# Expert weights in buffers of gathered rows: a separate chain of weight loads in a mixture-of-experts stage

## The chip, the cores and the metric

The kernel runs on one NeuronCore of a Trainium2 chip. The metric is the device time of one execution in microseconds. The kernel before takes 3864.81 us, the median of 3 runs (3861.73 to 3865.3). One more execution was profiled; it took 3860.75 us.

The engines of the core each work through their own list of instructions in order and wait for each other with semaphores: TensorE (PE) for matrix products and transposes, VectorE (DVE), ScalarE (ACT), GpSimd (POOL), which here issues all indexed transfers (gathers and scatters of rows), and SyncE (SP), which issues the plain transfers.

## The reference

Four layers follow each other on the same graph: 3125 nodes with 256 features, 50,000 edges. Each layer adds a graph part and then a feed-forward part to x. The change lies in the third layer (and, in part, in the fourth):

```python
x = x + _L2_gnn_ref(_layernorm(x), edge_attr_64, node_vec1, src, dst, W_self, W_func, W_att)
x = x + _L2_ffn_ref(_layernorm(x)[None], gate_w, gate_b, w1, b1, w2, b2, gamma, beta)[0]
```

The graph part is attention over edges. With z = h·W_func, an edge's score is a leaky ReLU of a linear function of z[src], z[dst] and an edge value; a softmax over the edges of each target node gives the weights with which the rows z[src] are summed; then come W_self, a ReLU and the sum with h. The feed-forward part is a mixture of 16 experts, of which each node takes 2:

```python
topk_vals, topk_idx = top_k(x @ gate_w + gate_b, 2);  topk_w = softmax(topk_vals)
h = relu(einsum('bsh,ehf->bsef', x, w1) + b1)          # f = 512
y = x + sum_k topk_w[k] * (h @ w2 + b2)[expert topk_idx[k]]
out = (y - mean(y)) / sqrt(var(y) + 1e-5) * gamma + beta
```

The fourth layer's graph part projects x with a ReLU, takes the maximum over each node's incoming edges, and adds two products and a batch norm; its feed-forward part is again a mixture, of 8 experts, 2 for each node. All is float32.

## The kernel before, in words

**Tiles.** The nodes are sorted by their number of edges and cut into 25 tiles of 128. The features of all of them stay in on-chip memory (`X`, `XX`, `ACC`). The gathered edge rows don't: an edge row is 258 floats, and one POOL instruction (`gather`, recorded at L136) fetches one row for each of 128 nodes. Tile t takes `RND[t]` such gathers; all tiles together take 413.

**The third layer's stage** (L2099 to L2303) has five strands, each a Python generator that yields the engine and an estimated duration of its next piece:

- `gathers()` on POOL fetches the edge rows for the tiles in `order2` (24 down to 6, then 0 to 5) into tiles named `g_rows`, four gathers each, in nine buffers (`GR_BUFS`), that is room for 36 gathers. A buffer comes free when DVE has added its last row (L2222).
- `attend()` does the softmax and the weighted sum of each tile, mainly on DVE.
- `route2()` does norm, gate logits, top 2 and positions in six groups, and scatters each node's row to its two experts' places in a table `xg` in HBM (POOL, L140).
- `ex2.loads()` on SP fetches tokens and weights for the experts.
- `experts2()` runs the experts chunk by chunk. Chunk 0 is tiles 15 to 24, chunk 1 tiles 6 to 14, chunk 2 tiles 0 to 5, the last to be gathered. Each chunk runs all 16 experts on a fixed number of places (2 × 96 in the first two, 128 in the last): transposes of the tokens (L1989, copied to `ro_xt` at L1994 on ACT or L1997 on DVE), the first product `mm` (L1947), the activation into `ro_h`, the second product `y` (L1951) and a store to the table `yg` in HBM (L2033).

After that a flag is read back and a branch taken if an expert's places overflowed (`ex2.rest`, L2036; here none do). Then `ex2.fetch` gathers each node's two results from `yg` (buffers `ro_g`, a ring of six), and `table3` in six groups of tiles (20–24, 15–19, 10–14, 6–9, 3–5, 0–2) combines them (L2093), norms, projects on PE for the fourth layer (L1734, L2265, L2267), applies the ReLU and scatters the rows to a table `tab3`, from which the fourth layer gathers. The end of chunk 2's experts and all of this run interleaved.

**What sets the order.** A list scheduler (`Plan`) walks the strands and writes all engines' instructions down in an order of its own, from the estimated durations, the ranks of the strands and objects that stand for buffers (`Ring`) and moments (`At`, `All`). The estimate only decides the order. Once written, each engine executes its list in that order, and real semaphores guard the data.

**The loads before.** For each chunk and expert, `loads()` (L1953) issues on SP, as one chain: the tokens (L1962), once a token buffer is free (`XR`, two) and all of the chunk's scatters are out (`sent[c]`); then the two halves of the expert's weights (L1968), 514 and 512 KB, each once one of its two buffers (`W_BUFS`) is free. So a chunk's first weights stand behind its first tokens. The fourth layer's stage (experts in chunks of tiles 0–4, 5–14 and 15–24) uses the same method.

Of the kernel before, what the change touches and what calls it, by code (L numbers as in the profile page):

```python
# [9 lines left out]
F32 = mybir.dt.float32  # L10
# [9 lines left out]
P = 128  # L20
# [4 lines left out]
D = 256  # L25
# [8 lines left out]
GB = 4  # L34
GR_BUFS = 9
ROWS = 24
W_BUFS = 2
GT = 5
# [26 lines left out]
ZW = D + 2  # L65
# [30 lines left out]
def tile_gnn_ffn(ctx: ExitStack, tc: tile.TileContext, a: dict, out: bass.AP):  # L96
    nc = tc.nc
# [1509 lines left out]
    X, XN = XX[:, :, V_X : V_X + D], XX[:, :, V_N : V_N + D]  # L1607
    ACC = np_.tile([P, NT, D], F32, name="ACC")
    xi = np_.tile([P, NT], I32, name="xi")
    lg2 = np_.tile([P, GT, 16], F32, name="lg2")  # L1610

    def turned(dst, src, scale=None, bias=None):

# [135 lines left out]
    plan = [None]  # L1749
# [60 lines left out]
    class Experts:  # L1810
# [3 lines left out]
        def __init__(self, key, n, act, chunks, pool, xg, yg, scale=None, bias=None):  # L1814
            self.n, self.act, self.chunks, self.pool, self.xg, self.yg = n, act, chunks, pool, xg, yg
            self.scale, self.bias = scale, bias
            self.f, self.fc, self.blocks = 512, 512 // P, a[key + "_blocks"]
            self.b2 = pool.tile([n, D], F32, name="ro_b2")
            nc.sync.dma_start(self.b2, a[key + "_b2"])

            self.base, self.trash = [], []
            for c, (t0, t1, m, k) in enumerate(chunks):
                e = pool.tile([P, n], F32, name=f"ro_e{c}")
                nc.vector.tensor_scalar(e, iota_f[:, :n], float(m * k), float(n * m * k), op0=OP.mult, op1=OP.subtract)
                tr = pool.tile([P, 2, t1 - t0], F32, name=f"ro_t{c}")
                nc.vector.tensor_scalar(tr.rearrange("p i t -> p (i t)"), iota_f[:, : 2 * (t1 - t0)], float(P), iota_p,
                                        op0=OP.mult, op1=OP.add)
                self.base.append(e)
                self.trash.append(tr)
            self.big = max(P, *(q[2] * q[3] for q in chunks))  # L1830
            self.bk = max(q[3] for q in chunks)
            self.back = pool.tile([P, 2, NT], I32, name="ro_back")
            self.pos = pool.tile([P, 2, NT], I32, name="ro_pos")
            self.w = pool.tile([P, 2, NT], F32, name="ro_w2")
            self.left = pool.tile([P, NT, n], F32, name="ro_left")
            self.sofar = [pool.tile([P, n], F32, name=f"ro_r{c}") for c in range(len(chunks))]
            for r in self.sofar:
                nc.vector.memset(r, 0.0)
            self.over = pool.tile([P, 1], F32, name="ro_over")
            nc.vector.memset(self.over, 0.0)  # L1840
            self.W, self.XR = (Ring(W_BUFS), Ring(W_BUFS)), Ring(2)
            self.there, self.came = [], [At() for _ in range(len(chunks) * n)]
            self.sent = [All(t1 - t0) for t0, t1, _, _ in chunks]
            self.made = [At() for _ in chunks]
            self.G, self.got, self.back_in = Ring(6), [[] for _ in range(NT)], [At() for _ in range(NT)]
            self.placed = [At() for _ in range(NT)]
# [103 lines left out]
            for i in range(self.fc):  # L1950
                nc.tensor.matmul(py, h[:, i, s], w[:, i * D : (i + 1) * D], start=(i == 0), stop=(i == self.fc - 1))  # L1951

        def loads(self):  # L1953

            pool, half = self.pool, 2 * self.f + self.fc
            for c, (_, _, m, k) in enumerate(self.chunks):
                for e in range(self.n):
                    r0 = e * m * k
                    f = yield "SP", 0.45, (self.XR, self.sent[c])
                    xfree = self.XR.take()  # L1960
                    x = pool.tile([P, self.bk, D], F32, name="ro_x", bufs=2)[:m, :k]
                    nc.sync.dma_start(x, self.xg[c][r0 : r0 + m * k, :].rearrange("(k p) d -> p k d", p=m))  # L1962
                    parts = [(x, plan[0].moved(f, m * k * 1024), xfree)]
                    for i, ring in enumerate(self.W):
                        f = yield "SP", 0.45, (ring,)
                        wfree = ring.take()
                        w = pool.tile([P, half if i == 0 else self.fc * D], F32, name=f"ro_w{i}", bufs=W_BUFS)
                        nc.sync.dma_start(w, self.blocks[e * P : (e + 1) * P, half * i : half + i * self.fc * D])  # L1968
                        parts.append((w, plan[0].moved(f, 0.53e6), wfree))
                    self.there.append(parts)  # L1970
                    self.came[len(self.there) - 1].t = f

        def run(self, c, R):

            pool, (_, _, m, k) = self.pool, self.chunks[c]
            cols = m * k

            def turn(e):
                at = c * self.n + e
                while self.came[at].t is None:  # L1980
                    yield None, 0.0, (self.came[at],)
                x, xl, xfree = self.there[at][0]
                xt = pool.tile([P, 2, self.big], F32, name="ro_xt", bufs=2)[:, :, :cols]
                for q in range(2):
                    f = yield "PE", 0.13 * k, (xl, R["tp"])
                    free = R["tp"].take()
                    pt = ps("tp", [P, 512])
                    for i in range(k):
                        nc.tensor.transpose(pt[:, i * m : (i + 1) * m], x[:, i, q * P : (q + 1) * P], ident[:m, :m])  # L1989
                    if q:  # L1990
                        xfree.t = f
                    f = yield ("ACT" if self.scale is not None else ("ACT", "DVE")), 0.15 + cols * 0.0011, (f,)
                    if self.scale is not None:
                        nc.scalar.activation(xt[:, q, :], pt[:, :cols], AF.Identity, bias=self.bias[:, q : q + 1],  # L1994
                                             scale=self.scale[:, q : q + 1])
                    else:
                        (nc.scalar.copy if plan[0].on == "ACT" else nc.vector.tensor_copy)(xt[:, q, :], pt[:, :cols])  # L1997
                    free.t = f
                return xt, f

            xt, xf = yield from turn(0)
            for e in range(self.n):
                (w1, wl1, free1), (w2, wl2, free2) = self.there[c * self.n + e][1:]
                h = pool.tile([P, self.fc, self.big], F32, name="ro_h", bufs=2)[:, :, :cols]
                for i in range(self.fc):
                    f = yield "PE", 2 * cols * MM_COL, (wl1, xf, R["mm"])
                    free = R["mm"].take()
                    ph = ps("mm", [P, 512])[:, :cols]
                    self.hidden(w1, xt, ph, i)
                    f = yield "ACT", 0.2 + cols * 0.0011, (f,)  # L2010
                    j = 2 * self.f + i
                    nc.scalar.activation(h[:, i, :], ph, self.act, bias=w1[:, j : j + 1])  # L2012
                    free.t = f
                hf = free1.t = f
                if e + 1 < self.n:
                    xt, xf = yield from turn(e + 1)
                y = pool.tile([P, self.bk, D], F32, name="ro_y", bufs=2)[:m, :k]
                for i0 in range(0, k, 2):
                    g = min(2, k - i0)
                    for i in range(g):  # L2020
                        f = yield "PE", self.fc * D * MM_COL, (hf, wl2, *((R["y"],) if i == 0 else ()))
                        if i == 0:
                            free = R["y"].take()
                            py = ps("y", [P, 2, D])[:m, :g]
                        self.out_of(py[:, i, :], w2, h, slice((i0 + i) * m, (i0 + i + 1) * m))
                    if i0 + g == k:
                        free2.t = f
                    f = yield ("ACT", "DVE"), 0.15 + 0.27 * g, (f,)
                    (nc.scalar.copy if plan[0].on == "ACT" else nc.vector.tensor_copy)(y[:, i0 : i0 + g, :], py)  # L2029
                    free.t = f  # L2030
                r0 = e * cols
                f = yield "SP", 0.45, (f,)
                nc.sync.dma_start(self.yg[c][r0 : r0 + cols, :].rearrange("(k p) d -> p k d", p=m), y)  # L2033
            self.made[c].t = f + 0.5
# [64 lines left out]
    with tc.tile_pool(name="g2", bufs=2) as gp, \  # L2099
# [179 lines left out]
        with tc.manual_schedule(engines={EN.PE, EN.DVE, EN.Activation, EN.Pool, EN.SP}):  # L2279
            pl.add(2, gathers())  # L2280
            pl.add(0, attend())
            pl.add(1, route2())
            pl.add(0, ex2.loads())
            last = pl.add(4, experts2())
            pl.run(moved, R.values())
            ex2.rest(range(NT))
# [11 lines left out]
    with tc.tile_pool(name="w3", bufs=1) as wp:  # L2298
# [70 lines left out]
        with tc.tile_pool(name="f3", bufs=1) as fp, psums(tp=2, mm=2, y=2, u=2):  # L2369
# [50 lines left out]
            with tc.manual_schedule(engines={EN.PE, EN.DVE, EN.Activation, EN.Pool, EN.SP}):  # L2420
                for i, q in enumerate(groups3):
                    befores.append(At())
                    pl.add(i, route3(*q, f"f{i % 2}_", befores[i], befores[i + 2]))
                pl.add(0, ex3.loads())
                pl.add(1.5, experts3())
                pl.run(routed, R.values())
                ex3.rest(range(NT))
# [59 lines left out]
```

## Time and profile before

| | |
|---|---|
| median of 3 runs | 3864.81 us |
| profiled execution: its time, its span | 3860.75 us, 3859.0 us |
| busy share of the span: PE, DVE, POOL, ACT | 71%, 51%, 45%, 22% |
| mean granted clock of PE | 0.82 |
| third layer: last gather of edge rows starts | 2709.32 us |
| third layer: chunk 2's tokens are loaded from | 2749.82 us |
| third layer: chunk 2's last expert output ends on PE | 2882.2 us |
| third layer: last scatter to the fourth layer's table ends | 2936.65 us |
| fourth layer: first gather of edge rows | 2943.27 us |
| fourth layer: first tokens loaded | 3515.13 us |

Times within the execution are microseconds from the start of its span. Busy time of an engine doesn't count waits or the issuing of plain transfers. A line of the timeline gives start, length, engine and source line, what it writes and reads, and in brackets how long the engine was idle before it and what ended that.

### The profile page before, as it was taken

The page shows a single profiled execution, that of the slowest core. Times are in us where ns is not written, and L with a number is a line of the kernel's source. Part 1 is how long each engine was busy: PE and PEld are TensorE (multiplying, and loading weights), DVE is VectorE, ACT ScalarE, POOL GpSimd, SP SyncE. Part 2 cuts the span into 40 slices and gives each one's busy share as a digit, 9 for nine tenths or more (in the row PEclk, how much of TensorE's full clock was granted, in tenths as well). Part 3 has the DMA queues.
Part 4 walks back from the last instruction along what each step waited for, and adds up shares of the span by engine and source line. Part 5 has one row for each costly group of instructions (what it writes and reads, how often), then busy time and mean ns, then how long its engine had stood idle before and what let it go on. Part 6 is the DMA issues. An engine that isn't in the chain of part 4 may idle for free. (4 is left out here: it accounts for less than half of the span.)

```text
span 3859.0 us, 46777 instructions
## 1 busy us (share of the span) xinstructions
PE 2721.7 (71%) x13015; PEld 2250.7 (58%) x13015; DVE 1987.3 (51%) x7555; ACT 846.0 (22%) x1771; POOL 1724.6 (45%) x1971
## 2 busy tenths in 40 slices
PE   3788999999899999999384227748483112237994
PEld 2666788887788888887373115537361111225673
DVE  4446665776566555544423755656664333337411
ACT  2111232322122322323121002213231000014331
POOL 0342233352144333330024777777435777762343
PEclk9778999998899999999687557869695555557997
DMA  5756544553243444431122437768452333333563
GB/s 181 235 157 208 165 136 128 153 159 84 67 120 94 137 115 122 116 109 47 49 87 73 110 104 241 212 185 261 161 172 76 105 105 105 105 93 116 172 212 97
DMA packets 274479, 518.31 MB, mean 134 GB/s; under 512 B 53068, under 2 KB 176106, under 8 KB 274194
## 3 DMA queue, kind: packets, MB, share of 16 engines
q0 software_dynamic: 103744, 303.34, 26.9%
q1 hardware_dynamic: 159598, 201.27, 16.9%
q10 hardware_dynamic: 10852, 10.45, 0.8%
q8 instruction: 113, 1.85, 0.2%
q14 instruction: 172, 1.41, 0.1%
HBM read 428.07 MB, written 86.78 MB: 133 GB/s over the span
## 5 line engine op out<-in xcount | busy, mean ns | idle before, releaser
L136 POOL DMA_INDIRECT g<-tab,m_si x521 | 499.1, 958 | 1013.7 <-PE agg L884 262.4
L136 POOL DMA_INDIRECT g_rows<-tab,srcI x413 | 401.7, 973 | 130.6 <-issue 101.8
L136 POOL DMA_INDIRECT g_row<-tab,srcI x413 | 391.0, 947 | 132.2 <-issue 118.1
L866 PEld LDWEIGHTS c<-s,g 128*128 128x128 f32 x2084 | 332.5, 207 | 95.6 <-issue 38.7
L897 PE MATMUL f<-w_rel,aT 128*126 128x256 f32 x1600 | 377.2, 385 | 0.0
L866 PE MATMUL c<-s,g 128*128 128x96 f32 x2084 | 334.2, 286 | 51.2 <-DMA g<-tab,m_si 21.6
L870 ACT COPY aT<-c 128x384 f32<-128x384 f32 (+1 forms) x273 | 230.0, 842 | 607.0 <-PE c L866 573.4
L873 PE MATMUL pw<-w_d,f 65*128 65x256 f32 x1042 | 354.1, 424 | 0.0
L2342 DVE TENSOR_TENSOR ACC<-ACC,g_row 128x256 f32<-128x256 f32 x413 | 175.7, 425 | 341.5 <-DMA g_row<-tab,srcI 340.9
L884 PE MATMUL agg<-g,s 128*126 128x256 f32 x1042 | 334.1, 403 | 5.4 <-DVE g L875 5.4
L897 PEld LDWEIGHTS f<-w_rel,aT 128*126 128x126 f32 x1600 | 302.3, 191 | 48.3 <-issue 4.0
L1617 PE MATMUL tp<-ident,ACC 128*128 128x128 f32 x50 | 16.6, 435 | 422.3 <-DVE ACC L2342 422.3
L1947 PE MATMUL mm<-ro_xt,ro_w 128*128 128x192 f32 (+3 forms) x1152 | 265.0, 378 | 46.8 <-ACT ro_h L2012 25.0
L875 DVE TENSOR_TENSOR g<-pw,g 128x256 f32<-128x256 f32 x521 | 218.9, 420 | 120.0 <-PE pw L873 117.5
L1951 PE MATMUL y<-ro_w,ro_h 128*96 128x256 f32 (+2 forms) x1152 | 267.3, 384 | 0.0
L1617 PEld LDWEIGHTS tp<-ident,ACC 128*128 128x128 f32 x50 | 7.2, 204 | 429.8 <-issue 354.1
L1947 PEld LDWEIGHTS mm<-ro_xt,ro_w 128*128 128x128 f32 x1152 | 200.6, 205 | 95.0 <-ACT ro_h L2012 33.0
L884 PEld LDWEIGHTS agg<-g,s 128*126 128x126 f32 x1042 | 211.4, 203 | 40.2 <-DVE g L875 5.8
L1951 PEld LDWEIGHTS y<-ro_w,ro_h 128*96 128x96 f32 (+2 forms) x1152 | 200.2, 179 | 43.5 <-issue 1.0
L1015 PE MATMUL w<-w,b_h 128*126 128x256 f32 x800 | 211.7, 389 | 3.5 <-ACT xt L928 1.7
L1006 PE MATMUL w<-xt,w 128*128 128x252 f32 (+1 forms) x832 | 206.8, 372 | 3.0 <-ACT b_h L1008 1.3
L2222 DVE SCALAR_TENSOR_TENSOR ACC<-g_rows,g_e,ACC 128x256 f32<-128x256 f32 x413 | 201.5, 488 | 13.6
(582 smaller groups left out, 4674.2 us busy)
## 6 DMA issues: line engine op xcount, KB each, us to landing
ro_w<-in_L_ffn_blocks SPq DMA_DIRECT2D x72, 514.0 KB
ro_w<-in_L_ffn_blocks SPq DMA_DIRECT2D x72, 512.0 KB
f<-in_attr_t SPq DMA_DIRECT2D x521, 32.5 KB
xg<-zero SPq DMA_DIRECT2D x78, 200.0 KB
b_at<-in_edge_attr SPq DMA_DIRECT2D x100, 125.0 KB
tabr<-v SPq DMA_DIRECT2D x12, 758.0 KB
g<-tab,m_si POOLq DMA_INDIRECT x521
g_rows<-tab,srcI POOLq DMA_INDIRECT x413
```

What stands on the lines that cost most here:

```text
L136: return nc.gpsimd.indirect_dma_start(out=dst, out_offset=None, in_=table, in_offset=bass.IndirectOffsetOnAxis(ap=idx, axis=0))
L866: nc.tensor.matmul(pc[:, h, o : o + GW], g[:, h * P : (h + 1) * P], sums[k][0], start=True, stop=True)
L870: nc.scalar.copy(aT[:, :, :, b : b + n * GN].rearrange("p k r n -> p k n r"), pc[:, :, : n * GW].rearrange("p k (n r) -> p k n r", r=16))
L873: nc.tensor.matmul(pw, feats.pop(k), wd, start=True, stop=True)
L875: nc.vector.tensor_tensor(g[:, D:], pw, g[:, D:], op=OP.mult)
L884: nc.tensor.matmul(cur["agg"][:TN], sums.pop(k)[1], rows.pop(k)[:, D:], start=(j == 0), stop=last)
L897: nc.tensor.matmul(cur["f"][:TN], aT[:, h, r, :], wrel[:, h, r, :], start=(r == 0 and h == 0), stop=(r == 15 and h == 1))
L1006: nc.tensor.matmul(ph, w["01"][:, e, k, i * P : (i + 1) * P], xt[:, k, : n * TN], start=(k == 0), stop=(k == 1))
L1015: nc.tensor.matmul(py, last[:, k, i * TN : (i + 1) * TN], w["02"][:, e - 1, k, :], start=(k == 0), stop=(k == 1))
L1947: nc.tensor.matmul(ph, w[:, o : o + P], xt[:, k, :], start=(k == 0), stop=(k == 1))
L1951: nc.tensor.matmul(py, h[:, i, s], w[:, i * D : (i + 1) * D], start=(i == 0), stop=(i == self.fc - 1))
L2222: stt(u, g[:, r, :D], e[:, r0 + r : r0 + r + 1], u, op0=OP.mult, op1=OP.add)
```

## The change

The loads are cut into two strands. `tokens()` issues the token loads, with the same conditions as before. `weights()` issues the weight loads, which wait only for a buffer: no longer for the tokens of the same expert, nor for the chunk's scatters. `run()` waits, in the plan, for each of the two separately.

For the third layer, `weights()` is given a second source of buffers: in the last chunk, from the third expert on, each half goes into a tile of the name `g_rows`, viewed as 128 × 1032 floats and cut to the half's width. In the plan such a load waits for a buffer of that ring and for the moment when the last row gather was issued (`here[order2[-1]]`). That gives 28 loads into nine buffers, about 4.5 experts deep, beside the two experts in the ordinary buffers. The fourth layer calls `weights()` without it. A tile of logits that nothing used is gone.

```diff
-        def loads(self):
-
-            pool, half = self.pool, 2 * self.f + self.fc
+        def tokens(self):
+
             for c, (_, _, m, k) in enumerate(self.chunks):
                 for e in range(self.n):
-                    r0 = e * m * k
+                    r0, at = e * m * k, c * self.n + e
                     f = yield "SP", 0.45, (self.XR, self.sent[c])
-                    xfree = self.XR.take()
-                    x = pool.tile([P, self.bk, D], F32, name="ro_x", bufs=2)[:m, :k]
+                    free = self.XR.take()
+                    x = self.pool.tile([P, self.bk, D], F32, name="ro_x", bufs=2)[:m, :k]
                     nc.sync.dma_start(x, self.xg[c][r0 : r0 + m * k, :].rearrange("(k p) d -> p k d", p=m))
-                    parts = [(x, plan[0].moved(f, m * k * 1024), xfree)]
-                    for i, ring in enumerate(self.W):
-                        f = yield "SP", 0.45, (ring,)
-                        wfree = ring.take()
-                        w = pool.tile([P, half if i == 0 else self.fc * D], F32, name=f"ro_w{i}", bufs=W_BUFS)
-                        nc.sync.dma_start(w, self.blocks[e * P : (e + 1) * P, half * i : half * i + self.fc * D])
-                        parts.append((w, plan[0].moved(f, 0.53e6), wfree))
-                    self.there.append(parts)
-                    self.came[len(self.there) - 1].t = f
+                    self.there[at] = x, plan[0].moved(f, m * k * 1024), free
+                    self.came[at].t = f
+
+        def weights(self, more=None):
+
+            half = 2 * self.f + self.fc
+            for c in range(len(self.chunks)):
+                for e in range(self.n):
+                    for i in range(2):
+                        n = (half, self.fc * D)[i]
+                        if more and c + 1 == len(self.chunks) and e >= W_BUFS:
+                            ring, make, since = more
+                            f = yield "SP", 0.45, (ring, since)
+                            w = make()[:, :n]
+                        else:
+                            ring = self.W[i]
+                            f = yield "SP", 0.45, (ring,)
+                            w = self.pool.tile([P, n], F32, name=f"ro_w{i}", bufs=W_BUFS)
+                        free = ring.take()
+                        nc.sync.dma_start(w, self.blocks[e * P : (e + 1) * P, half * i : half * i + n])
+                        at = (c * self.n + e) * 2 + i
+                        self.loaded[at] = w, plan[0].moved(f, 0.53e6), free
+                        self.fetched[at].t = f
...
-            pl.add(0, ex2.loads())
+            pl.add(0, ex2.tokens())
+            pl.add(0, ex2.weights((blocks, lambda: gp.tile([P, GB, ZW], F32, name="g_rows", bufs=GR_BUFS)
+                                   .rearrange("p r d -> p (r d)"), here[order2[-1]])))
...
-                pl.add(0, ex3.loads())
+                pl.add(0, ex3.tokens())
+                pl.add(0, ex3.weights())
```

More of the change, by code (lines that the diff above doesn't have):

```diff
@@ L1609, in tile_gnn_ffn @@
     xi = np_.tile([P, NT], I32, name="xi")
-    lg2 = np_.tile([P, GT, 16], F32, name="lg2")
     def turned(dst, src, scale=None, bias=None):
@@ L1841, in __init__ @@
             self.W, self.XR = (Ring(W_BUFS), Ring(W_BUFS)), Ring(2)
-            self.there, self.came = [], [At() for _ in range(len(chunks) * n)]
+            self.there, self.came = {}, [At() for _ in range(len(chunks) * n)]
+            self.loaded, self.fetched = {}, [At() for _ in range(2 * len(chunks) * n)]
             self.sent = [All(t1 - t0) for t0, t1, _, _ in chunks]
@@ L1962, in loads @@
                     nc.sync.dma_start(x, self.xg[c][r0 : r0 + m * k, :].rearrange("(k p) d -> p k d", p=m))
-                    parts = [(x, plan[0].moved(f, m * k * 1024), xfree)]
-                    for i, ring in enumerate(self.W):
-                        f = yield "SP", 0.45, (ring,)
-                        wfree = ring.take()
-                        w = pool.tile([P, half if i == 0 else self.fc * D], F32, name=f"ro_w{i}", bufs=W_BUFS)
-                        nc.sync.dma_start(w, self.blocks[e * P : (e + 1) * P, half * i : half + i * self.fc * D])
-                        parts.append((w, plan[0].moved(f, 0.53e6), wfree))
@@ L1981, in turn @@
                     yield None, 0.0, (self.came[at],)
-                x, xl, xfree = self.there[at][0]
+                x, xl, xfree = self.there.pop(at)
                 xt = pool.tile([P, 2, self.big], F32, name="ro_xt", bufs=2)[:, :, :cols]
@@ L2002, in run @@
             for e in range(self.n):
-                (w1, wl1, free1), (w2, wl2, free2) = self.there[c * self.n + e][1:]
+                at = (c * self.n + e) * 2
+                while self.fetched[at + 1].t is None:
+                    yield None, 0.0, (self.fetched[at + 1],)
+                (w1, wl1, free1), (w2, wl2, free2) = self.loaded.pop(at), self.loaded.pop(at + 1)
                 h = pool.tile([P, self.fc, self.big], F32, name="ro_h", bufs=2)[:, :, :cols]
```

## The prediction

> **What bounds the kernel now.** I began with the page's busy tenths and costliest groups, to see which engine is late in the third layer, then took ten-microsecond windows, and then the timelines of PE, DVE, POOL and SP around the three places where an expert chunk starts. The group of row gathers:
>
> ```profile
> L136 POOL DMA_INDIRECT g_rows<-tab,srcI x413 | 401.7, 973 | 130.6 <-issue 101.8
> ```
>
> The 413 gathers are 0.97 us of POOL each, and the idle before them is mostly issue: until the last one POOL sets the pace, one gather in 1.25 us. Then comes a lull. Windows (start:end, length, then PE, PEld, DVE, ACT, POOL busy, granted clock, DMA share, GB/s):
>
> ```profile
> 2720.00:2730.00 10.00, 0.00 (x0) 0.00 (x0) 9.24 (x27) 0.00 (x0) 1.44 (x4) 0.50 0.07 26
> 2730.00:2740.00 10.00, 4.17 (x17) 3.31 (x17) 4.36 (x27) 2.04 (x5) 0.00 (x0) 0.50 0.00 1
> 2740.00:2750.00 10.00, 3.20 (x7) 1.16 (x6) 3.77 (x28) 0.51 (x2) 5.13 (x8) 0.50 0.18 59
> 2750.00:2760.00 10.00, 4.15 (x18) 3.81 (x19) 2.14 (x5) 1.37 (x4) 7.56 (x9) 0.50 0.86 293
> 2760.00:2770.00 10.00, 7.28 (x40) 6.03 (x38) 2.62 (x6) 2.89 (x9) 7.41 (x7) 0.93 0.93 297
> 2770.00:2780.00 10.00, 6.50 (x29) 6.10 (x30) 9.39 (x38) 3.07 (x9) 5.54 (x6) 0.66 0.51 169
> ```
>
> The last gather is followed by attention on the last tile, its norm and its routing, all serial on DVE, while the DMA engines rest for 25 us (shares 0.07, 0.00). Then, from 2750, weights, tokens and the return gathers of the finished chunks all run together at 0.86 to 0.93. On POOL the last row gather, and the last four token scatters after their wait for the routing:
>
> ```profile
> 2709.32 0.94 POOL L136 DMA_INDIRECT g_rows<-tab,srcI  x1 [0.30 <-issue]
> 2743.43 0.97 POOL L140 DMA_INDIRECT xg<-XX,ro_pos  x1 [21.80 <-ACT ro_ct L1934]
> ```
>
> What that burst costs PE (start, length, instruction, idle before and its releaser):
>
> ```profile
> 2752.67 0.66 PE L1989 MATMUL tp<-ident,ro_x 128*128 128x128 f32 x2 [8.68 <-DMA ro_x<-xg]
> 2756.51 3.76 PE L1947 MATMUL mm<-ro_xt,ro_w 128*128 128x128 f32 x16 [3.18 <-DMA ro_w<-in_L_ffn_blocks]
> 2773.50 3.38 PE L1947 MATMUL mm<-ro_xt,ro_w 128*128 128x128 f32 x14 [6.13 <-DVE ro_xt L1997]
> 2794.16 0.69 PE L1734 MATMUL tp<-ident,XX 128*128 128x128 f32 x2 [4.59 <-ACT XX L1779]
> ```
>
> and DVE, which caused the 6.13:
>
> ```profile
> 2767.27 0.48 DVE L2093 SCALAR_TENSOR_TENSOR ACC<-ro_g,ro_w,ACC 53x256 f32<-53x256 f32 x1 [3.86 <-DMA ro_g<-yg,ro_back]
> 2770.12 0.48 DVE L2093 SCALAR_TENSOR_TENSOR ACC<-ro_g,ro_w,ACC 53x256 f32<-53x256 f32 x1 [2.38 <-DMA ro_g<-yg,ro_back]
> ```
>
> The first product waits 3.18 us for weights. The last two return gathers of the first group, issued by POOL at 2759.2 and 2761.2, reach DVE only at 2767 and 2770, eight us later, where a quiet one takes about 2.4; DVE stands, and PE behind it. The page's chain of waits covers only the end of the program, so I use it for nothing. From 2750 to 2936.65 (the last table scatter) PE is busy for 135 us and DVE for 116, nearly all of it the six table groups, about 24 per five tiles. The stage thus ends on a chain of both: last expert output (2882.2), return gathers, norm, product, scatter.
>
> [...] the gathers of POOL and the weights of SP shared 2750 to 2772 (24.9% and 61.6% of engine time by queue), and the gathers were late. [...] sixteen passes took 3.76 us at 2756 (clock 0.50) and 2.22 at 2779.
>
> **The change, part by part.** The sum is against the profiled execution (3860.75 us, span 3859.0); the median of the runs, 3864.81, lies 4 above and takes the same difference.
>
> *Counts.* Nothing is computed differently. SP issues the same 144 weight and 72 token loads; bytes are equal. The removed logits tile had no instruction: 0. In the new instruction order, two experts' weights of chunk 0 go to SP ahead of the edge loop; the first four halves of each later chunk stand among the last output stores of the chunk before; for chunk 2, nine more halves go into gathered-row buffers, ahead of the overflow branch; later halves follow 4.5 experts ahead.
>
> *(a) Chunk 1's start.* Before, token and weight loads went out together at 2561.3 to 2564.5; PE waited 2.00 for weights, row gathers of that time came late (DVE waited 4.44), and POOL then waited 4.97 for a buffer (2576.06), its only long stall from there to its last gather. With weights already resident, a wait near the usual 1.3 is left: −3.7. Bounds −5 (all of it) and 0 (the burst, now earlier, stalls POOL elsewhere).
>
> *(b) End of the gathers.* Four halves into ordinary buffers and about four of the nine fall into 2700 to 2712: 8 × 0.52 = 4.2 MB less what lands after the last gather, some 2.6 MB, or 6 us at the 405 GB/s of 2755 to 2760, 9 at the 297 above. The last gather stands on the path. The return gathers above were 6 late in a longer burst; I take +2.5, bounds 0 and +6.
>
> *(c) Chunk 2 with weights there.* PE's first product starts after its tokens alone, 3.0 earlier (2753.5). Without the first weights' burst the last return gather of group 0 should land near 2763, not 2770, so DVE's group and PE's first table tile come about 7 earlier (2787 for 2794.2). In the new PE order two more experts (seven, not five) stand ahead of the first table tile, so the expert stream doesn't wait for that tile (4.59) and three fewer tiles stand before the last output. An expert is 2.22 + 0.38 + 1.89, 4.25 start to start with overlap; a table tile is 2.2 (0.38 + 0.69 + 1.13). The last output then ends at 2882.2 − 7 − 2 × 4.25 − 3 × 2.2 = 2860 for 2882.2: −22. Check against plain work: 16 × 4.25 + 13 × 2.2 = 97 us from 2753.5 is 2850, so 10 us of stalls are still allowed.
>
> *(d) The tail.* Before, 54.5 us pass from the last output to the last table scatter: return gathers from
>
> ```profile
> 2886.01 0.98 POOL L136 DMA_INDIRECT ro_g<-yg,ro_back  x1 [0.31 <-issue]
> 2935.68 0.97 POOL L140 DMA_INDIRECT tab<-ACC,idI  x1 [2.34 <-ACT ACC L2270]
> ```
>
> and two groups of three tiles. Now the three tiles left over fall to PE's tail at half clock, and DVE runs the two last groups one wholly after the other, where before the second's sums stood in the first's gaps. Gathers 2866 to 2873.5, in DVE at 2875.5 (also when DVE is free of the group before), first norm 2889.5, second 2906, then 15.2 to the last scatter as before: 2921. That gives back +6. Of each moved step, SP's queue is what is passed: outputs' stores wait behind weight loads whose buffers aren't free, but from chunk 2's start these are free 4.5 experts ahead, so 0; bound +4.
>
> *(e) Layer 3.* Its weights lose their tie to the tokens too. PE was 95% busy there and its first product waited for no DMA: 0, bounds −3 and +3. If that cover failed, the most would be a 2 to 3 us wait as at chunks 1 and 2.
>
> Sum: −3.7 + 2.5 − 22 + 6 = −17. Against the median: 3848.
>
> **Rivals.** *R1, contention only moves.* Weights of experts six onward stream while group 1's return gathers land; these are as late as the first's were, and the DVE and POOL chain of table groups (24 us per five tiles) keeps its end. For it: DVE's 116 us can't shrink. Against it: 2770 to 2936 is 166 us, and PE, not DVE, was dense (9.64 busy of 10 at 2810). Left are (a), (b) and half of the first 7: about −7, 3858.
> *R2, hidden.* The routing wait and the DVE chain decide all, the gain goes into the tail: ±2, 3865.
> *R3, slower: DVE held by its order.* DVE copies of tokens (ro_xt) are put in order by modelled load times. If a token's load is late there, DVE stands with norms and attention behind it. The trace has such holds of 11.71 us at chunk 1
>
> ```profile
> 2564.94 0.36 DVE L1997 COPY ro_xt<-tp 128x192 f32<-128x192 f32 x1 [11.71 <-PE tp L1989]
> ```
>
> and the new order has its copies placed for weights that come early. A second such hold before the last attention, 12 us, plus (b) at +6, less (a), takes back 14; beyond 17 us of new hold it is a loss, beyond 25 a measurable one. Price if it strikes fully: two holds of 12 and 6 of late gathers, +13: 3878. Against it: tokens' own gate (all scatters) is unchanged.
> *R4, larger.* The DVE chain moves with the first group by 7 and the tail keeps its overlap: −30, 3835.
> *That it doesn't do what it says* is nearly excluded: nine loads do stand ahead of the branch in the order.
>
> **How the numbers follow.** Forecast (3840 to 3857) 0.57; R4 0.09; R1 0.14, of which half is under 0.2%; R2 0.08; R3 0.12. 0.2% is 7.7 us, about what a measurement of this kernel can tell from no change: faster is below 3857.1, slower above 3872.5. Faster 0.57 + 0.09 + 0.07 = 0.73, same 0.07 + 0.08 + 0.01 = 0.16, slower 0.11. The range 3834 to 3866 leaves out R3 and the ends of R4 (0.04) and R2 (0.03), 0.19 together.
>
> **What would show it.** (a) no wait near 4.97 on POOL at chunk 1's start; (b) the last row gather within 6 us of 2709 and DVE's wait for it not above 6; DMA share over 0.5 just after 2710; (c) no DMA wait at the first product of chunk 2, the last return gather of group 0 near 2763, last output near 2860; (d) about 60 us from it to the last table scatter. Wrong it would be if DVE shows holds above 10 us at token copies or return gathers still come 6 late, or if layer 3 moves by more than 3.

## The result and the profile after

The changed kernel takes 3846.93 us, the median of 6 runs (3841.11 to 3849.48), against 3860.91 of 6 runs of the kernel before (3856.71 to 3865.3). The ratio is 0.9961 with a 95% interval of 0.9948 to 0.9974, so 15 us faster, between 10 and 20. The forecast was 3848 against 3864.81, 17 less. Differences in microseconds are worked out from the ratio here and below; those of the medians lie up to 3 us beside them.

The profiled execution has a span of 3847.8 us, 11.2 below the one before. I lay both out from fixed points of the trace, in microseconds:

| stretch | before | after | difference |
|---|---|---|---|
| start to the third layer's first row gather | 2093.4 | 2094.4 | +1.0 |
| first to last row gather | 615.9 | 611.6 | −4.3 |
| last row gather to chunk 2's first transpose | 43.35 | 46.54 | +3.2 |
| that to chunk 2's first product | 3.84 | 0.80 | −3.0 |
| that to the first table tile on PE | 37.65 | 39.54 | +1.9 |
| that to the last expert output's end | 88.19 | 71.84 | −16.4 |
| that to the last table scatter's end | 54.30 | 57.73 | +3.4 |
| that to the fourth layer's first gather | 6.62 | 6.63 | 0 |
| that to the end of the span | 915.73 | 918.67 | +2.9 |

From the first row gather to the fourth layer's first gather that is −15.2. One term, −16.4, is larger than the whole: the stretch in which chunk 2's experts and the table tiles (table3's tiles of nodes) share PE. The others add up to +1.2.

The windows of the kernel after (columns as before) show the burst of early weights, around the last row gather and in the lull behind it:

```profile
2700.00:2710.00 10.00, 1.22 (x8) 0.55 (x6) 6.57 (x39) 1.07 (x3) 5.59 (x7) 0.72 0.81 255
2710.00:2720.00 10.00, 4.56 (x9) 1.76 (x9) 6.45 (x25) 1.10 (x5) 4.47 (x8) 0.50 0.51 175
2720.00:2730.00 10.00, 1.19 (x2) 0.49 (x2) 9.34 (x28) 0.12 (x1) 4.85 (x9) 0.50 0.89 323
2750.00:2760.00 10.00, 7.27 (x29) 6.47 (x30) 3.22 (x8) 2.00 (x6) 7.56 (x9) 0.55 0.46 146
2760.00:2770.00 10.00, 8.08 (x53) 6.94 (x51) 3.97 (x12) 4.37 (x13) 7.87 (x8) 1.00 0.57 168
```

The load is moved: 323 GB/s in 2720 to 2730 where there were 26, and a DMA share of 0.46 in 2750 to 2760, where it was 0.86. PE is busy for 7.27 of those ten, before 4.15.

On POOL and DVE, the last row gather and what waits for it:

```profile
2706.05 0.95 POOL L136 DMA_INDIRECT g_rows<-tab,srcI  x1 [0.30 <-issue]
```
```profile
2713.06 0.22 DVE L2219 SCALAR_TENSOR_TENSOR g_e<-g_rows,XX,ewF 128x3 f32<-128x3 f32 x1 [5.03 <-DMA g_rows<-tab,srcI]
2765.51 0.47 DVE L2109 SCALAR_TENSOR_TENSOR ACC<-ro_g,ro_w,ACC 53x256 f32<-53x256 f32 x1 [2.75 <-DMA ro_g<-yg,ro_back]
2767.65 0.48 DVE L2109 SCALAR_TENSOR_TENSOR ACC<-ro_g,ro_w,ACC 53x256 f32<-53x256 f32 x1 [1.66 <-DMA ro_g<-yg,ro_back]
```

Before, that wait was:

```profile
2712.72 0.25 DVE L2203 SCALAR_TENSOR_TENSOR g_e<-g_rows,XX,ewF 128x3 f32<-128x3 f32 x1 [1.17 <-DMA g_rows<-tab,srcI]
```

The last gather starts 3.3 us earlier than before, but its rows reach DVE no earlier (2713.06, before 2712.72; DVE's wait for them is 5.03 and was 1.17). And the last return gathers of the first table group are still about 6 us on their way. On PE:

```profile
2753.39 3.79 PE L1947 MATMUL mm<-ro_xt,ro_w 128*128 128x128 f32 x16
2771.24 3.04 PE L1947 MATMUL mm<-ro_xt,g_rows 128*128 128x128 f32 x16 [3.09 <-DVE ro_xt L2010]
2792.39 0.70 PE L1951 MATMUL y<-g_rows,ro_h 128*128 128x256 f32 x2 [2.17 <-ACT ro_h L2028]
2792.93 0.42 PE L1733 MATMUL tp<-ident,XX 128*128 128x128 f32 x2
```

The first product waits for nothing. The wait behind DVE's token copy is 3.09 (before 6.13), and the first table tile comes at 2792.93 (before 2794.16), with seven experts ahead of it, where there were five.

### The profile page after: what moved, and what is told of

Read it like the earlier page. It is cut to its first block, busy times and chain, and to the rows that moved or that the text cites. A ratio compares the mean times of both kernels' runs of the same rounds, so it can differ in the third digit from the quotient of the medians.

```text
span 3847.8 us, 46812 instructions
## 1 busy us (share of the span) xinstructions
PE 2731.5 (71%) x13015; PEld 2259.5 (59%) x13015; DVE 1988.4 (52%) x7554; ACT 848.3 (22%) x1772; POOL 1725.3 (45%) x1971
## 5 line engine op out<-in xcount | busy, mean ns | idle before, releaser
L1947 PE MATMUL mm<-ro_xt,ro_w 128*128 128x192 f32 (+3 forms) x928 | 232.8, 401 | 29.9 <-ACT ro_h L2028 24.0
L1951 PE MATMUL y<-ro_w,ro_h 128*96 128x256 f32 (+2 forms) x1040 | 243.3, 388 | 0.0
L1947 PEld LDWEIGHTS mm<-ro_xt,ro_w 128*128 128x128 f32 x928 | 171.5, 207 | 74.9 <-ACT ro_h L2028 30.9
L1951 PEld LDWEIGHTS y<-ro_w,ro_h 128*96 128x96 f32 (+2 forms) x1040 | 181.4, 179 | 41.7 <-issue 1.3
```

The lines of the kernel that those rows point to most:

```text
L1947: nc.tensor.matmul(ph, w[:, o : o + P], xt[:, k, :], start=(k == 0), stop=(k == 1))
```

## The experiments

Theory S, supply: weights that are there earlier and 4.5 experts deep let the experts run. Theory O, order: the planner prices a weight half at 0.53 MB over 180 GB/s, 2.9 us, so it took chunk 2 for bound by its loads, 5.9 us an expert. Told that weights are there earlier, it writes two more experts ahead of the first table tile, and these fill waits that PE had anyway. The first four kernels ran with shared runs of the kernel before (median 3864.53 of 40), the next four likewise (3865.13 of 11).

**Split chains alone**, no row buffers:

```diff
-            pl.add(0, ex2.weights((blocks, lambda: gp.tile([P, GB, ZW], F32, name="g_rows", bufs=GR_BUFS)
-                                   .rearrange("p r d -> p (r d)"), here[order2[-1]])))
+            pl.add(0, ex2.weights())
```

> The chains are split in both layers, but no weights go into row buffers. In its order one more expert (six, not five) stands ahead of the first table tile; in the changed kernel it is two more. Theory S (supply: early and deep weights let the experts run): the first product of chunk 2 has its weights, 3 us, and later experts wait for weights as before; about -3 us. Theory O (order: the planner, told that weights come sooner, puts more experts ahead of the first table tile, where PE otherwise waits): one of two experts' worth, 4.25 of 8.5, plus 3 of the first product, less the tail's give-back: -5 to -9 us.

Measured: ratio 0.9978 (0.9968 to 0.9988), −8.5 us. It lies at O's side: one more expert is ahead of the table tile, and that is what both the order and the time show. From last row gather to chunk 2's first transpose it needs 43.2 us, as before; the first product follows after 0.8.

**Order alone**: the kernel before, with the planner's price of chunk 2's weights halved.

```diff
-                        parts.append((w, plan[0].moved(f, 0.53e6), wfree))
+                        fast = self.n == 16 and c == 2
+                        parts.append((w, plan[0].moved(f, 0.53e6 / (2.0 if fast else 1.0)), wfree))
```

> The kernel before, loads in one chain and two buffers as they were; only the planner is told that chunk 2's weights take half the modelled time. Its PE order then has seven experts ahead of the first table tile, as the changed kernel has. Theory S: experts five and six come no sooner, since their weights wait for two buffers; 0, or slower by a few us. Theory O: weights at 1.05 MB per 4.25 us are 247 GB/s, which the chip moved here, so the order alone brings 8.5 of experts in PE's waits less the tail's 3: -7 to -11 us.

Measured: 0.9976 (0.9967 to 0.9986), −9.3 us. No load was untied, no buffer added. The order isn't wholly the changed kernel's: seven experts stand ahead of the first table tile in both, but here 15 tiles stand before the last output, 14 in the changed kernel and 17 before. PE in chunk 2 of this kernel (timeline; the lines with a wait):

```profile
2761.33 3.75 PE L1947 MATMUL mm<-ro_xt,ro_w 128*128 128x128 f32 x16 [2.74 <-DMA ro_w<-in_L_ffn_blocks]
2774.75 0.44 PE L1990 MATMUL tp<-ident,ro_x 128*128 128x128 f32 x2 [0.80 <-DMA ro_x<-xg]
2778.66 2.82 PE L1947 MATMUL mm<-ro_xt,ro_w 128*128 128x128 f32 x16 [1.75 <-DVE ro_xt L1998]
2799.22 0.70 PE L1951 MATMUL y<-ro_w,ro_h 128*128 128x256 f32 x2 [1.88 <-ACT ro_h L2013]
```

After the first weights (2.74 us) PE waits for weights nowhere: two buffers feed experts at this pace. From the first table tile to the last output it takes 75.1 us (88.2 before), and its tail (from there to the last table scatter) is 58.6 (54.3): both halves of the trade come with the order.

**Old order**, with the early weights and the row buffers kept; the planner is told the pace of the old chain (in `tokens()` it books each expert's weights on its modelled wire behind the tokens, and `run()` takes the later of that and the true load):

```diff
+            self.late = {}
...
+                    if self.n == 16 and c == 2:
+                        self.late[e] = [plan[0].moved(f + 0.45 * i, 0.53e6) for i in (1, 2)]
...
-                        self.loaded[at] = w, plan[0].moved(f, 0.53e6), free
+                        self.loaded[at] = w, f if self.n == 16 and c == 2 else plan[0].moved(f, 0.53e6), free
...
+                if self.n == 16 and c == 2:
+                    wl1, wl2 = max(wl1, self.late[e][0]), max(wl2, self.late[e][1])
```

> The changed kernel with its early and deep weights, but the planner is told that chunk 2's weights come at the pace of the old chain; its PE order has five experts ahead of the first table tile, as before. Theory S: most of the gain stays, -9 to -14 us. Theory O: only the earlier start of the first product is left, and PE then waits for the table tile: -1 to -4 us.

Measured: 0.9990 (0.9984 to 0.9997), −3.9 us. PE of this kernel:

```profile
2770.01 3.37 PE L1948 MATMUL mm<-ro_xt,g_rows 128*128 128x128 f32 x14 [7.23 <-DVE ro_xt L2013]
2790.66 0.69 PE L1733 MATMUL tp<-ident,XX 128*128 128x128 f32 x2 [4.59 <-ACT XX L1778]
```

The weights lie there and PE stands: 7.23 for DVE's token copy and, as in the kernel before, 4.59 for the first table tile. Early weights start the experts 3.0 us sooner, and PE waits that out: from chunk 2's first transpose to its last output 129.2 us pass, 129.7 before. So early and deep weights bring 0.5 there in the old order, and the rest of the −3.9 must come from elsewhere, such as chunk 1's start (below). Theory S fails for the main part.

**Fourth layer tied again**: the changed kernel with one chain for tokens and weights in the fourth layer (`tied()`, not shown, issues them as the kernel before did).

```diff
-                pl.add(0, ex3.tokens())
-                pl.add(0, ex3.weights())
+                pl.add(0, ex3.tied())
```

> The changed kernel with the fourth layer's loads back in one chain with the tokens. In the profiles the fourth layer's experts, from first tokens to last output, took 294.6 us after and 291.1 before. If the split of the chains costs these 3.5 us there: about -17 us against the kernel before. If they are chance: -14, like the changed kernel.

Measured: 0.9963 (0.9951 to 0.9976), −14.3 us: the changed kernel's own ratio. From first tokens on PE (8 us after their load, from which the expectation counts) to the last output the fourth layer took 289.1 us in this profile, 283.0 before and 286.4 after, so nothing points to the split, and the 2.9 us of the table above are of the size by which executions differ.

**The 53-row tile first**, in the third layer: tile 24 holds 53 nodes, not 128; its return gathers were the last of the first group, and the late ones.

```diff
+        def short_first(tiles):
+            return sorted(tiles, key=lambda t: t != NT - 1)
...
-            ready = []
-            for t in tiles:
-                ready.append((yield from ex2.combine(t)))
+            ready = [None] * g
+            for t in short_first(tiles):
+                ready[t - t0] = yield from ex2.combine(t)
...
-            pl.add(3, ex2.fetch([t for g in order3 for t in range(*g)]))
+            pl.add(3, ex2.fetch([t for g in order3 for t in short_first(range(*g))]))
```

> The changed kernel, but the return gathers and the combining of the last node tile (53 rows, not 128) come first in their group, in the third layer only. Theory R (a 53-row gather takes some 6 us to land by its shape: 1.6 us on POOL, landing 5.7 after its issue also in the quiet end of the program): DVE no longer waits 2.75 and 1.66 us at the end of the group, the group ends about 4 us earlier and the stage with it; -17 to -19 us against the kernel before. Theory C (contention with weights, as the prediction had it): whatever is gathered last is late; -14, like the changed kernel.

Measured: 0.9956 (0.9940 to 0.9971), −17.0 us, not told apart from the changed kernel by its time. The trace shows the landing. POOL and DVE of this kernel:

```profile
2755.85 1.60 POOL L136 DMA_INDIRECT ro_g<-yg,ro_back  x1 [1.07 <-issue]
2757.76 1.58 POOL L136 DMA_INDIRECT ro_g<-yg,ro_back  x1 [0.30 <-issue]
```
```profile
2761.89 0.47 DVE L2109 SCALAR_TENSOR_TENSOR ACC<-ro_g,ro_w,ACC 53x256 f32<-53x256 f32 x1 [1.71 <-DMA ro_g<-yg,ro_back]
2763.69 1.11 DVE L2109 SCALAR_TENSOR_TENSOR ACC<-ro_g,ro_w,ACC 53x256 f32<-53x256 f32 x2 [1.32 <-DMA ro_g<-yg,ro_back]
2771.48 0.48 DVE L2109 SCALAR_TENSOR_TENSOR ACC<-ro_g,ro_w,ACC 128x256 f32<-128x256 f32 x1 [0.92 <-DMA ro_g<-yg,ro_back]
2779.20 0.49 DVE L2109 SCALAR_TENSOR_TENSOR ACC<-ro_g,ro_w,ACC 128x256 f32<-128x256 f32 x1 [2.04 <-DMA ro_g<-yg,ro_back]
```

Gathered first, they still need 6.0 and 5.9 us from issue to DVE, while the group's last gather, now of 128 rows (issued at 2768.49), needs 3.0. So it is the shape and not the place in the queue. Counted from chunk 2's first transpose the group is complete 12.3 us later, in the changed kernel 15.1: 2.8 won. But the first table tile comes only 0.3 earlier (40.0 us after that transpose, 40.3): DVE has sums of the second group inside the first group's norm, as in the changed kernel, but here it stands 2.04 and 0.43 us for their gathers. DVE, whose sums stand in that order, gave back what its input had won.

**The burst held**: the first load into a row buffer waits for a memset of one column that DVE does after the last attention; the other eight queue behind it on SP.

```diff
-                            ring, make, since = more
-                            f = yield "SP", 0.45, (ring, since)
-                            w = make()[:, :n]
+                            ring, make, since, hold = more
+                            if (e, i) == (W_BUFS, 0):
+                                f = yield "DVE", 0.07, (ring, hold)
+                                w = make()[:, :n]
+                                nc.vector.memset(w[:, :1], 0.0)
+                                f = yield "SP", 0.45, (f,)
+                            else:
+                                f = yield "SP", 0.45, (ring, since)
+                                w = make()[:, :n]
...
-                                   .rearrange("p r d -> p (r d)"), here[order2[-1]])))
+                                   .rearrange("p r d -> p (r d)"), here[order2[-1]], done[order2[-1]])))
```

> The changed kernel, but the nine loads into row buffers are held until the last tile's attention is done (one 128x1 memset on DVE, on which the first of them depends). If the burst makes the last row gather late: DVE's wait for it falls from 5.03 to about 1.2 us, from the last gather's start to chunk 2's first transpose 43 us and not 46.5; -17 against the kernel before. If the wait has another cause: 46.5 as before, -14.

Measured: 0.9953 (0.9938 to 0.9967), −18.2 us. SP of this kernel:

```profile
2700.35 4.41 SPq L1987 DMA_DIRECT2D ro_w<-in_L_ffn_blocks  x2
2727.73 4.47 SPq L1987 DMA_DIRECT2D g_rows<-in_L_ffn_blocks  x9
```

All nine go out between 2727.7 and 2732.2, in the lull. DVE doesn't wait for the last row gather at all, and from last gather to first transpose it needs 43.5 us, not 46.5. The burst's 3 us are shown by that stretch; the time alone can't tell them, since the intervals overlap.

**Split chains, faster price, no row buffers**: the first experiment's kernel with the planner's price for chunk 2 halved, which gives the changed kernel's PE order in chunk 2.

```diff
-                        self.loaded[at] = w, plan[0].moved(f, 0.53e6), free
+                        self.loaded[at] = w, plan[0].moved(f, 0.53e6 / (2.0 if self.n == 16 and c == 2 else 1.0)), free
```

> The split chains with no row buffers (two weight buffers only), and the planner told that chunk 2's weights take half the modelled time; its PE order is the changed kernel's. Theory O (order and early first weights bring the gain, the row buffers nothing, and their burst costs 3): -15 to -18 us, 43 us from last gather to first transpose, and waits for weights on PE of under 2 us in chunk 2. Theory S (experts two to six need weights ahead): PE waits for weights there, -5 to -10.

Measured: 0.9950 (0.9935 to 0.9965), −19.3 us. DVE and PE of this kernel:

```profile
2712.53 0.22 DVE L2219 SCALAR_TENSOR_TENSOR g_e<-g_rows,XX,ewF 128x3 f32<-128x3 f32 x1 [0.89 <-DMA g_rows<-tab,srcI]
```
```profile
2766.72 1.97 PE L1951 MATMUL y<-ro_w,ro_h 128*128 128x256 f32 x8 [0.27 <-DMA ro_w<-in_L_ffn_blocks]
2772.98 3.53 PE L1947 MATMUL mm<-ro_xt,ro_w 128*128 128x128 f32 x16 [4.30 <-DVE ro_xt L2010]
```

Without row buffers PE waits 0.27 us for weights in all of chunk 2, and the last row gather's wait is 0.89. The change's own subject, the loads into freed buffers, is not needed for its gain.

One stretch sorts the kernels, from chunk 2's first transpose to the end of its last output: 129.7 us before, 129.2 with early and deep weights in the old order, 119.6 with split chains alone, 117.0 with the order alone, 112.2 in the changed kernel, 111.0 with split chains and the faster price.

**All of it**: the burst held, the 53-row tile first in the third layer, and in the fourth layer first among the last chunk's tiles in the final gathers and scatters.

```diff
+            order4 = [*range(15), NT - 1, *range(15, NT - 1)]
...
-                for t in range(NT):
+                for t in order4:
...
-                pl.add(0, ex3.fetch(range(NT)))
+                pl.add(0, ex3.fetch(order4))
```

> The changed kernel with the burst held, and the 53-row tile first in its group in the third layer, and first in the last chunk of the fourth layer's final gathers and scatters. With both theories right, 3 + 4 us in the third layer and about 4 at the program's end, where the last two gathers' waits of 4.99 and 1.36 us and a 1.57 us scatter stand: -23 to -26 against the kernel before. With neither: -14.

Measured: 3839.84 us, 0.9936 (0.9920 to 0.9952), −24.7 us: the lowest time of the study. Its interval still touches the changed kernel's. Its profile explains less: first row gather to fourth layer's first gather 830.1 us (after: 834.7), last output to the end of the program 51.5 (52.7, so 1.2 won for 4 expected); 5.7 us of the 10.7 between its profile and the changed kernel's lie ahead of the first row gather, where nothing was changed.

**The same without row buffers**: split chains and the faster price, with these tile orders.

> Split chains, two weight buffers only (no row buffers, so no burst), the planner told that chunk 2's weights take half the modelled time, and the 53-row tile first in its group in the third layer and first in the last chunk of the fourth layer's end. If the row buffers bring nothing: as fast as the kernel that has them with the burst held and the same tile orders, -18 to -25 us. If they do help once the groups end earlier: -12 to -17.

Measured: 0.9969 (0.9957 to 0.9981), −13.3 us, against a kernel before of 4300.96 us, 11% longer than elsewhere; it was another chip. POOL waited 163.4 us for row buffers in this kernel, where the first profile has 15.3, so chunk 2 met other surroundings. A second run, on a third chip:

> The same kernel as the one with split chains, two weight buffers, the faster modelled weights and the 53-row tile first, on another chip: the first took 4301 us for the kernel before, with row gathers that made POOL wait 163 us for buffers, so its chunk 2 stood in another place. If the row buffers bring nothing: -18 to -25 us; if they help: -12 to -17.

Measured: 0.9956 (0.9940 to 0.9971), −18.8 us, against 4273.41, again slow. It is a gain there too; whether it beats the held row buffers these two runs can't say.

**Chunks 0 and 1 alone**: no row buffers, and chunk 2's weights tied to its tokens again, so that order and supply of chunk 2 are as before.

```diff
-                            f = yield "SP", 0.45, (ring,)
+                            tie = (self.came[c * self.n + e],) if self.n == 16 and c == 2 else ()
+                            f = yield "SP", 0.45, (ring, *tie)
...
-            pl.add(0, ex2.weights((blocks, lambda: gp.tile([P, GB, ZW], F32, name="g_rows", bufs=GR_BUFS)
-                                   .rearrange("p r d -> p (r d)"), here[order2[-1]])))
+            pl.add(0, ex2.weights())
```

> Split chains for chunks 0 and 1 and in the fourth layer, while chunk 2's weights stay behind its tokens: old PE order, no burst, no earlier first product in chunk 2. It leaves only the early weights at the starts of chunks 0 and 1. By the prediction's step (a): -3.7 us. If that step was worth nothing: within 2 us of the kernel before.

Measured: 0.9993 (0.9977 to 1.0009), −3.0 us, on the first of the two slow chips.

> The same kernel as the one that splits chunks 0 and 1 alone, on another chip for the same reason. By the prediction's step (a): -3.7 us; if that step was worth nothing, within 2 us of the kernel before.

Measured: 0.9993 (0.9981 to 1.0005), −3.0 us, on the second. Twice near step (a), twice with an interval that holds zero (the medians differ by 5.6 and by 0.8): not proved by time, and where POOL waits up to 33.9 us for a row buffer, as in the first of these profiles, the start of chunk 1 isn't the one that the step is about. The profiles at normal speed say more. POOL's wait at chunk 1's start, before and after:

```profile
2576.06 1.08 POOL L136 DMA_INDIRECT g_rows<-tab,srcI  x1 [4.97 <-DVE ACC L2222]
```
```profile
2572.17 1.08 POOL L136 DMA_INDIRECT g_rows<-tab,srcI  x1 [1.94 <-DVE ACC L2238]
```

The order alone, where the loads are tied, has 5.17 there; the eight kernels with split loads have 2.33 at most. POOL's group of row gathers, before, after, split chains alone, order alone:

```profile
L136 POOL DMA_INDIRECT g_rows<-tab,srcI x413 | 401.7, 973 | 130.6 <-issue 101.8 <-DVE ACC L2222 15.3 <-DMA g_rows<-tab,srcI 4.3
```
```profile
L136 POOL DMA_INDIRECT g_rows<-tab,srcI x413 | 403.4, 977 | 127.5 <-issue 102.8 <-DVE ACC L2238 10.8 <-DMA g_rows<-tab,srcI 4.0
```
```profile
L136 POOL DMA_INDIRECT g_rows<-tab,srcI x413 | 403.4, 977 | 126.7 <-issue 102.8
```
```profile
L136 POOL DMA_INDIRECT g_rows<-tab,srcI x413 | 403.0, 976 | 130.8 <-issue 102.5
```

The idle before gathers is 130.6 and 130.8 us in the two kernels with tied loads and 126.5 to 127.9 in the eight with split ones; the part that DVE's release ends falls from 15.3 to 10.8. The whole stretch from first to last row gather is a poorer witness: with the burst held it is 615.8 us, as before, though that kernel's wait at chunk 1 is 1.62. POOL stands there 4.68 us ahead of a token scatter at 2455, which was 3.23 before and 0.19 in the changed kernel.

## Why the prediction was right, and where its steps were not

**(a) Chunk 1's start, −3.7:** right in kind, and near in size: POOL's wait there is 3.0 shorter (4.97, now 1.94), and DVE's wait for row gathers ahead of it 3.1 (4.44, now 1.33). First to last row gather is 4.3 shorter, but that holds another 3.0 from the wait ahead of the token scatter, which the step doesn't explain, less 1.8 more of POOL's own work.

**(b) The burst, +2.5:** measured +3.2; held, or without row buffers, it is gone (43.5, 43.2 and 42.9 us for 46.5).

**(c) Chunk 2.** First product, −3.0: measured −3.0. Two more experts and three fewer tiles ahead of the last output, −8.5 − 6.6 = −15.1: measured −16.4. The failed term is the −7 for the first table tile, which moved by 1.1 against the first transpose. The step read the late return gathers (eight us) as contention with weights. Most of it was their shape. The gathers of the same tile in the quiet end of the program before:

```profile
3846.26 0.48 DVE L2093 SCALAR_TENSOR_TENSOR ACC<-ro_g,ro_w,ACC 53x256 f32<-53x256 f32 x1 [4.97 <-DMA ro_g<-yg,ro_back]
3848.19 0.48 DVE L2093 SCALAR_TENSOR_TENSOR ACC<-ro_g,ro_w,ACC 53x256 f32<-53x256 f32 x1 [1.45 <-DMA ro_g<-yg,ro_back]
```

They were issued at 3840.51 and 3842.40, 5.75 and 5.8 us earlier. Both lines stood in the profile of before, with 53 in the shape that I quoted; I compared with a quiet gather of 128 rows, and put that at 2.4, where the two ahead of these took 2.8 and 2.9. The rest went with the load: 2761.23 to 2770.12 is 8.9 us, at a DMA share of 0.93 in 2760 to 2770, and in the changed kernel it is 6.1, at 0.57. So about 2.8 of the 7 were to be had, and 2.5 were (2767.65 for 2770.12). Of these, 1.1 reached PE: the norm's result is there 2.0 earlier (ACT begins to write XX at 2791.49, before at 2793.50), but in the new order the end of the seventh expert comes first, held by ACT behind that norm (the 2.17 above).

That PE's order shifts was in the step; what shifts it was not asked. The prediction named the planner's order as something to read off, not as the cause. The runs show it as the main cause: order alone −9.3, early weights in the old order −3.9, together 13.2 of the 15, if the two simply add.

**(d) The tail, +6:** measured +3.4, the mechanism as described: between DVE's sums of the last two groups 13.3 us pass, filled with the whole norm of the first, where it was 9.9, and PE's granted clock is 0.50 from 2880 to 2920. The last output ends at 2864.8 (2860 was said), the last table scatter at 2922.5 (2921).

**(e) The fourth layer, 0:** right as far as the runs tell; its +2.9 doesn't go away with the tied chain.

The −17 came near the −15 partly by errors that cancel: 5.9 us too much for the first table tile, against 2.6 too much given back in the tail and 1.1 that the other terms were short of together. That (a) comes out at −4.3 and not less is owed to the scatter's wait, so luck had a part there too.

The rivals: R1, contention only moved, was half true. The waits for the second group's gathers did remain (in the 53-row experiment they cost 2.5), but PE was dense enough for the order to pay. R3, long holds of DVE, did not grow here: the one at chunk 1 is 11.78 us (11.71 before), at chunk 2 8.39 (8.84). As a sign of being wrong, "holds above 10 us" was badly set, since one stood there already.

Two readings to set right: the prediction's shares of engine time by queue, 24.9% and 61.6%, belong to 2749 to 2772 (from 2750 they are 25.4% and 64.4%), and the second holds tokens and stores besides weights. A quiet return gather took 2.7 to 2.9 us from issue to DVE in that trace, not the 2.4 of the prediction. And beside the sixteen passes at clock 0.50 (3.76 us) belongs the clock of those that took 2.22 us: 1.00, in 2779 to 2782.

## What to carry to other kernels

Where a planner writes the order from modelled durations, a change to supply can also change the order, as it did here; test the order by itself, by changing only the price that the planner uses. Here a modelled load of half the price gave more than half of the gain, and no buffer was needed. And before a late transfer is put down to contention, look for the same shape in a quiet place of the same trace.

## What the runs showed of the hardware

A gather of 53 rows of 1 KB takes longer than one of 128: mostly 1.57 to 1.60 us on POOL (0.95 for 128 rows). From issue to its reader it needs 5.7 to 5.8 us in the quiet end of the program before (128 rows: 2.8 and 2.9), 5.9 to 6.1 beside chunk 2's loads in the changed kernel and in that with the tile first, and 8.1 and 8.9 in the burst before. What makes it slower was not shown: no view here counts the engines of a transfer. That such a gather runs on a single one of the 16 DMA engines is the author's estimate from rates: in the run with all orders the two such gathers of the program's end are issued at 3789.45 and 3791.35 with nothing else under way (they reach DVE 5.8 and 6.4 us later), and the rate of the DMA engines by slices of 0.2 us from 3789 to 3797 is

```profile
GB/s 0 0 0 0 0 0 0 0 0 0 0 0 0 4 27 23 24 0 0 0 20 41 21 27 24 45 22 20 27 184 143 287 82 41 20 123 184 205 184 26
```

some 25 GB/s for one of them, up to 45 where both run, and peaks of 184 to 287 once the 128-row gathers behind arrive. In 2755 to 2760 of the kernel before, at a DMA share of 1.03, 405 GB/s moved, over 16 engines also 25 for each. A gather of 128 rows with the spare ones ignored might remove it; that wasn't tried.

On two of the chips the kernel before took 4301 and 4273 us, with no profile of it there. In the profile of chunks 0 and 1 alone on the second of them, ACT stands 11.0 us ahead of an output copy in chunk 1 for a release that the profile can't place, and DVE 20.9 us at a token copy behind it. What makes them slow stays open.
